# A graph network's raw groups: normalised on VectorE instead of ScalarE, with their statistics taken once a group

## The chip, the cores and the metric

The kernel runs on one core of one Trainium2 chip. The metric is the device time of one execution in microseconds (us); lower is better. The engines are TensorE (PE in the views, its weight loads PEld), VectorE (DVE), ScalarE (ACT), GpSimd (POOL) and SyncE (SP). They run side by side, each in its own program order.

## The reference

One message-passing layer of a graph network with a GRU as the node update: 12500 nodes of 128 features, 400000 edges sorted by destination, 32 features an edge.

```python
h = jnp.maximum(_layernorm(x, axis=-1), 0.0)         # per node
m = relu(concat([h[src], h[dst], ea]) @ w1 + b1) @ w2 + b2
agg = segment_sum(m, dst)                            # 12500 x 128
gi = agg @ w_ih + b_ih;  gh = h @ w_hh + b_hh        # each split into r, z, n
r = sigmoid(i_r + h_r);  z = sigmoid(i_z + h_z);  n = tanh(i_n + r * h_n)
out = x + (1 - z) * n + z * h
```

## The kernel before

**Opening stage** (some 90 us): `x` is loaded in batches, normalised, transposed into `hT_all` (the whole `h`, feature-major, in SBUF), multiplied by the first third of `w1` and stored as the table `A` in HBM, so that for most edges `h[src] @ w1a` is one row of `A`. `B = h @ w1b + b1` is made the same way in batches of 448 nodes.

**Edge stage.** 3125 tiles of 128 edges are worked in 391 groups of 8 tiles (the first has 5), each in two units of 4 tiles: `NU = 782` units. The loop over units runs `stages(u)`, a software pipeline written out by hand: for unit u+3 `pre` multiplies one-hot columns (`L`) with rows of `B` (`RW`) into PSUM, for u+2 `add` adds the source rows, takes the relu and writes `RB` (VectorE, L748), and `seg(u)` multiplies `RB` by one-hot matrices to sum by destination. Every 14 groups a `node` generator does the GRU for a block of nodes, a step a unit.

Source rows reach a group in one of five ways:

- **Groups 0 to 8, "raw"** (`RAW = 9`, units 0 to 17, 69 tiles). `A` isn't stored yet, so GpSimd gathers rows of `x` itself while the opening stage runs. Unit by unit they go through `raw_stats` (VectorE: mean and variance, L227 and L229; ScalarE: the root, L234) at u+7, `raw_fin` (VectorE: six small operations for scale and bias, L240 to L247) and `raw_h` (ScalarE: relu and normalise, one instruction a tile, L292) at u+6, `raw_turn` at u+4 (TensorE transposes into the one PSUM bank `misc`, L699, VectorE copies it to `gt`, L701). `pre` multiplies `gt` by `w1a` (L727). Their relu into `RB` is ScalarE's (L760), once a group.
- **Most of the others**: GpSimd gathers rows of `A`, eight indirect DMAs a group (L170), into a ring of `GBUFS = 11` buffers `G`. A buffer is free when the transposes (raw) or the addition (`A` rows) that reads it are done.
- **31 groups "dve"**: VectorE copies columns of `hT_all` two at a time (`Pairs`, L1021, 512 instructions a group, with loads of addresses into registers between them). `pairs_due` spreads them evenly over the units from `START["dve"]` on; the same number sets which groups they are (18, 30, 42 and so on).
- **30 groups "act"**: ScalarE copies columns one by one (L1062, 1024 a group, spread by `run_jobs`; the first of them, group 11, from unit -6 on).
- **5 groups "sp"**: SyncE issues one small DMA a row.

So each engine's order around the change is fixed by the text of `stages`, by the due counts of the pairs and by the job shares of `run_jobs`; GpSimd's order is the ring.

Of the kernel before, what the change touches and what calls it, by code (L numbers as in the profile page):

```python
# [9 lines left out]
F32 = mybir.dt.float32  # L10
# [7 lines left out]
ALU = mybir.AluOpType  # L18
# [5 lines left out]
GRP = 4  # L24
PAIR = 2 * GRP
# [19 lines left out]
RAW = 9  # L45
# [9 lines left out]
QUEUE = 10  # L55
ROW = 4 * D
SPREAD = {"dve": 31, "act": 30, "sp": 5}
START = {"dve": 8, "act": -6, "sp": 8}
NR = 12672

H_AT = 16512
# [3 lines left out]
def tile_gnn(ctx: ExitStack, tc: tile.TileContext, x, src, srcT, dstT, dstP, eaT, eaP, w1, b1, w2T, b2,  # L65
             wih, bih, whh, bhh, out):
    nc = tc.nc
# [5 lines left out]
    p2 = ctx.enter_context(tc.tile_pool(name="p2", bufs=2))  # L73
# [4 lines left out]
    ps1 = ctx.enter_context(tc.tile_pool(name="ps1", bufs=1, space=bass.MemoryType.PSUM))  # L78
# [7 lines left out]
    def unit_tiles(u):  # L86
        k, h = divmod(u, 2)
        t0, t1 = tiles(k)
        return [(t0 + a * GRP + j, j, a) for j in (2 * h, 2 * h + 1) for a in range(2)
                if t0 + a * GRP + j < t1]  # L90

    mode, order = {}, {m: [] for m in SPREAD}
    for m, n in SPREAD.items():
        lo, hi = START[m] // 2 + 2, NP - {"dve": 5, "act": 3, "sp": 12}[m]
        for i in range(n):
# [32 lines left out]
    ident = const.tile([128, 128], F32, name="ident")  # L128
# [94 lines left out]
    def bn(pool, xs, P, n):  # L223
        b = pool.tile([128, 8, 6], F32, name="bn")
        mv = pool.tile([128, 8, 2], F32, name="mv")
        for j in range(n):
            nc.vector.bn_stats(b[:P, j, :], xs(j))  # L227
        for j in range(n):
            nc.vector.bn_aggr(mv[:P, j, :], b[:P, j, :])  # L229
        return mv  # L230

    def bn_sqrt(pool, mv, P, n):
        s = pool.tile([128, 8], F32, name="s")
        nc.scalar.activation(s[:P, :n], mv[:P, :n, 1], AF.Sqrt, bias=eps[:P, :])  # L234
        return mv, s

    def bn_fin(pool, st, mvs, P, n):
        mv, s = mvs
        y = pool.tile([128, 8], F32, name="y")
        nc.vector.reciprocal(y[:P, :n], s[:P, :n])  # L240
        v = pool.tile([128, 8], F32, name="v")
        nc.vector.tensor_scalar(v[:P, :n], mv[:P, :n, 1], 1e-5, -0.5, op0=ALU.add, op1=ALU.mult)
        nc.vector.tensor_tensor(v[:P, :n], v[:P, :n], y[:P, :n], op=ALU.mult)
        nc.vector.tensor_tensor(v[:P, :n], v[:P, :n], y[:P, :n], op=ALU.mult)
        nc.vector.scalar_tensor_tensor(st[:P, :n, 0], v[:P, :n], 1.5, y[:P, :n],
                                       op0=ALU.add, op1=ALU.mult)
        nc.vector.scalar_tensor_tensor(st[:P, :n, 1], mv[:P, :n, 0], -1.0, st[:P, :n, 0],  # L247
                                       op0=ALU.mult, op1=ALU.mult)
# [42 lines left out]
    def relu_norm(o, xi, st):  # L291
        nc.scalar.activation(o, xi, AF.Relu, bias=st[:, 1:2], scale=st[:, 0:1])  # L292
# [90 lines left out]
    with tc.tile_pool(name="pp", bufs=3) as pp:  # L383
# [22 lines left out]
        mvs, asb = {}, {}  # L406
# [186 lines left out]
    Ls, OH, RT, HE, SEG = ({} for _ in range(5))  # L593
# [14 lines left out]
    def onehot_T(k):  # L608
        if k >= NP:
            return  # L610
        c = slice((k % QP) * 512, (k % QP + 1) * 512)
        o, i = Ls[k // QP][:2 * V, c], Ls[k // QP].bitcast(I32)[:2 * V, c]
        n = k - BLOCKS[-1][0]
        if n < 0:
            nc.vector.tensor_scalar(o, i, node_of[:, k:k + 1], None, op0=ALU.is_equal)  # L615
        else:
            nc.vector.tensor_scalar(o, i, node_of[:, k:k + 1], 0.0, op0=ALU.is_equal, op1=ALU.add,
                                    accum_out=dlast[:2 * V, n:n + 1])
# [50 lines left out]
    def unit(u):  # L669
        k, h = divmod(u, 2)  # L670
        return G[k][:, 2 * h:2 * h + 2, :, :].rearrange("p j a f -> p (j a) f")


    def slots(u):
        return [(j % 2) * 2 + a for _, j, a in unit_tiles(u)]

    def raw_h(u):
        if u < 2 * RAW:
            for i, s in enumerate(slots(u)):
                relu_norm(unit(u)[:, s, :], unit(u)[:, s, :], HE[u][:, i, :])  # L680

    def raw_stats(u):
        if u < 2 * RAW:
            l = slots(u)
            HE[u] = bn_sqrt(p2, bn(p2, lambda j: unit(u)[:, l[j], :], 128, len(l)), 128, len(l))

    def raw_fin(u):
        if u < 2 * RAW:
            n = len(slots(u))
            st = p2.tile([128, GRP, 2], F32, name="st_raw", bufs=4)  # L690
            bn_fin(p2, st[:, :n, :], HE[u], 128, n)
            HE[u] = st

    def raw_turn(u):
        if u < 2 * RAW:
            l = slots(u)
            pt = ps1.tile([128, 512], F32, name="misc")
            for i, s in enumerate(l):
                nc.tensor.transpose(pt[:, i * 128:(i + 1) * 128], unit(u)[:, s, :], ident)  # L699
            hT = p3.tile([128, 512], F32, name="gt", bufs=3)  # L700
            nc.vector.tensor_copy(hT[:, :len(l) * 128], pt[:, :len(l) * 128])  # L701
            HE[u] = hT

    PP = {}
# [1 line left out]
    def pre(u):  # L706
        if u >= NU:
            return
        k, h = divmod(u, 2)
        if h == 0:  # L710
            PP[k] = ps2.tile([128, PAIR, D], F32, name="pre")
        p = PP[k][:, GRP * h:GRP * h + GRP, :]
        for i in range(2):
            c0 = (k % QP) * 512 + (2 * h + i) * 128
            raw = u in HE or k in hand
            nc.tensor.matmul(p[:, 2 * i:2 * i + 2, :], Ls[k // QP][:, c0:c0 + 128], RW[k % 4],  # L716
                             start=True, stop=not raw)
            if raw:
                l = unit_tiles(u)
                for n, (t, j, a) in enumerate(l):  # L720
                    if j % 2 == i:
                        if k in hand:
                            c = (a * GRP + j) * 128
                            cols = hand[k][:, c:c + 128]
                        else:
                            cols = HE[u][:, n * 128:(n + 1) * 128]
                        nc.tensor.matmul(p[:, 2 * i + a, :], cols, w1a, start=False,  # L727
                                         stop=n + 1 == len(l) or l[n + 1][1] != j)
# [28 lines left out]
    def relu(u):  # L757
        if u in RT:
            o, p = RT.pop(u)
            nc.scalar.activation(o, p, AF.Relu)  # L760
# [308 lines left out]
    def pairs_due():  # L1069
        start, n = START["dve"], 0  # L1070
        for k in order["dve"]:
            end = 2 * k - 6
            for u in range(start, end):
                due[u] = n + -(-(PAIR * 64 * (u + 1 - start)) // (end - start))
            n += PAIR * 64
            start = end
# [3 lines left out]
    def behind(u):  # L1080
        return due.get(u, cols.end if u >= START["dve"] else 0) - cols.done

# [4 lines left out]
    def before_long(u, ops):  # L1087
        if u == START["dve"]:
            cols.load()
        some(u, cols.end, QUEUE - ops)  # L1090
        if cols.turn and u % 2 == 0:
            some(u, cols.end, QUEUE - ops - 1)
            cols.part()

    def behind_long(u, least):
        if behind(u) >= least:
            cols.pairs(cols.left())
            cols.load()
# [9 lines left out]
    for m in ("act", "sp"):  # L1108
        start = START[m]
        for k in order[m]:  # L1110
# [39 lines left out]

    def stages(u):
        if u + 7 >= 0:
            raw_stats(u + 7)
        if u + 6 >= 0:
            raw_fin(u + 6)
            raw_h(u + 6)
        if u + 4 >= 0:
            raw_turn(u + 4)
        if u + 3 >= 0:
            pre(u + 3)  # L1160
        before_long(u, 2 if u % 4 == 2 else 1)
        if u % 2 == 0:
            onehot_T(u // 2 + 3)
            onehot(u // 2 + 3)
        if u + 2 >= 0:
            add(u + 2)
            relu(u + 2)
        behind_long(u, 1)

    nc.vector.tensor_scalar(at[:ROWS, :], at[:ROWS, :], place_of[:, 0:1], place_of[:, 1:2],  # L1170
                            op0=ALU.mult, op1=ALU.add)
    for u in range(-7, 0):
        run_jobs(u, 0)
        stages(u)
        for phase in range(1, PH):
            run_jobs(u, phase)
# [16 lines left out]
    for u in range(NU):  # L1193
        k, h = divmod(u, 2)
        gathers(u)
        if h == 0:
# [14 lines left out]
            if k == NP - 20:  # L1211
                check_windows()
        run_jobs(u, 0)
        stages(u)
        run_jobs(u, 1)
        some(u, 4, QUEUE - 1)
# [188 lines left out]
```

## Time and profile before

| | |
|---|---|
| three timed runs | 3355.47, 3372.85, 3372.74 us; median 3372.74 |
| the profiled execution | 3356.5 us; its span 3354.7 us |
| ACT busy | 3232.5 us, 96% of the span |
| POOL busy | 2509.1 us, 75%, 2606 instructions |
| DVE busy | 2429.4 us, 72% |
| PE busy | 2383.9 us, 71%; mean granted clock 0.812 |

Busy shares leave out the loads of registers and the sequencers' own time between two instructions; the views call idle time in which nothing was waited for "issue". So an engine at 75% can be without a pause. The raw groups lie between about 90 and 230 us; everything after them is the long even part, and the last 30 us are the close.

### The profile page before, as it was taken

How to read it: one execution, taken by the hardware profiler on the slowest of the kernel's cores; microseconds unless marked ns; L12 is line 12 of the kernel's file. 1: busy time of each engine (PE TensorE's matmuls, PEld its weight loads, DVE VectorE, ACT ScalarE, POOL GpSimd, SP SyncE). 2: the span in 40 equal slices, each digit the busy share in tenths (PEclk: the TensorE clock that was granted, in tenths of full speed). 3: DMA queues.
4: the chain of work that ended last, by engine and by line, in shares of the span. 5: the costliest groups of instructions: out<-in, count | busy, mean ns of one | idle time of the engine just before them, and what ended most of it. 6: DMA issues, size and time to landing. Idle time of an engine off the chain costs nothing. (4 is left out here: it accounts for less than half of the span.)

```text
span 3354.7 us, 98027 instructions
## 1 busy us (share of the span) xinstructions
PE 2383.9 (71%) x13209; PEld 1538.6 (46%) x13209; DVE 2429.4 (72%) x18411; ACT 3232.5 (96%) x31050; POOL 2509.1 (75%) x2606
## 2 busy tenths in 40 slices
PE   7567777766776777677677676776776676767767
PEld 6444444444444454444444444444444444434444
DVE  8467777777767777777777777767777777777775
ACT  6899999999999999999999999999999999999996
POOL 7657777777777777777777777777777777777776
PEclk9777887878877888778888878877887888888888
DMA  6323444444444443434444344444444434444332
GB/s 212 100 69 84 104 98 102 93 103 99 99 94 100 96 99 94 105 90 98 101 97 100 94 101 99 96 93 101 97 98 100 102 96 95 99 99 100 92 97 72
DMA packets 195246, 332.94 MB, mean 99 GB/s; under 512 B 68682, under 2 KB 117385, under 8 KB 194587
## 3 DMA queue, kind: packets, MB, share of 16 engines
q0 software_dynamic: 83104, 170.36, 23.3%
q1 hardware_dynamic: 111339, 156.21, 17.1%
q14 instruction: 549, 4.50, 0.4%
q8 instruction: 110, 1.80, 0.2%
q10 hardware_dynamic: 144, 0.07, 0.0%
HBM read 306.13 MB, written 20.24 MB: 97 GB/s over the span
## 5 line engine op out<-in xcount | busy, mean ns | idle before, releaser
L1062 ACT COPY HE_act<-hT_all 128x4 uint8 x30720 | 3094.2, 189 | 56.7 <-issue 29.6
L170 POOL DMA_INDIRECT G<-A,src_i x2528 | 2442.0, 966 | 806.0 <-issue 747.7
L1021 DVE SCALAR_TENSOR_TENSOR both<-hT_all 128x4 uint16 x15872 | 1353.8, 153 | 693.6 <-issue 653.6
L716 PE MATMUL pre<-RW,L 128*128 128x256 f32 x3128 | 1101.7, 476 | 9.5 <-DMA RW<-B 9.5
L774 PE MATMUL seg<-RB,OH 128*32 128x129 f32 x6250 | 599.7, 322 | 627.5 <-DVE RB L748 477.6
L716 PEld LDWEIGHTS pre<-RW,L 128*128 128x128 f32 x3128 | 646.3, 231 | 284.3 <-issue 213.1
L774 PEld LDWEIGHTS seg<-RB,OH 128*32 128x32 f32 x6250 | 330.9, 124 | 920.0 <-DVE RB L748 550.9
L748 DVE CUSTOM_DVE_ANT_0 RB<-pre,G 128x1024 f32<-128x1024 f32 (+1 forms) x317 | 383.2, 1209 | 32.0 <-PE pre L716 19.0
L615 DVE TENSOR_SCALAR L<-L,node_of 64x512 f32<-64x512 int32 x382 | 186.7, 489 | 12.0 <-DMA L<-in_dstP 12.0
L666 DVE TENSOR_TENSOR OH<-dloc,seg 128x512 f32<-128x512 f16 (+1 forms) x198 | 131.1, 662 | 0.0
L851 PE MATMUL nd<-DEG,brow 34*128 34x512 f32 (+2 forms) x112 | 72.0, 726 | 82.8 <-ACT gt L861 81.2
L806 PE MATMUL misc<-spot_h,dcol 128*128 128x40 f16 x382 | 47.4, 192 | 88.3 <-DVE dcol L831 86.3
L801 PE MATMUL nd<-spot,sums 128*128 128x40 f32 x782 | 98.7, 290 | 14.2 <-DVE sums L783 12.3
L1032 DVE COPY HE_dve<-both 128x512 uint8<-128x512 uint8 x248 | 107.5, 434 | 0.0
L801 PEld LDWEIGHTS nd<-spot,sums 128*128 128x128 f32 x782 | 93.9, 198 | 22.0 <-DVE sums L783 13.0
L727 PEld LDWEIGHTS pre<-w1a,HE_dve 128*128 128x128 f32 x496 | 87.1, 220 | 9.8
L727 PEld LDWEIGHTS pre<-w1a,HE_act 128*128 128x128 f32 x480 | 84.4, 219 | 14.2 <-ACT HE_act L1062 4.7
L727 PE MATMUL pre<-w1a,HE_act 128*128 128x128 f32 x480 | 84.3, 303 | 4.1 <-ACT HE_act L1062 4.1
L727 PE MATMUL pre<-w1a,HE_dve 128*128 128x128 f32 x496 | 86.1, 302 | 0.0
L806 PEld LDWEIGHTS <-dcol 128*128 128x128 f16 x382 | 38.8, 105 | 101.9 <-DVE dcol L831 93.8
L170 POOL DMA_INDIRECT G<-in_x,src_i x69 | 65.6, 951 | 22.2 <-issue 20.7
L743 DVE TENSOR_SCALAR RB<-pre 128x1024 f32<-128x1024 f32 x61 | 74.0, 1213 | 4.7 <-PE pre L727 4.6
(180 smaller groups left out, 1389.0 us busy)
## 6 DMA issues: line engine op xcount, KB each, us to landing
G_sp<-A SPq DMA_DIRECT2D x5120, 0.5 KB
L<-in_dstP SPq DMA_DIRECT2D x195, 256.0 KB
L<-in_eaP SPq DMA_DIRECT2D x195, 256.0 KB
G<-A,src_i POOLq DMA_INDIRECT x2528, 2.5
RW<-B SPq DMA_DIRECT2D x782, 16.0 KB
xb<-in_x SPq DMA_DIRECT2D x26, 256.0 KB
out<-xb SPq DMA_DIRECT2D x26, 256.0 KB
xs<-in_x SPq DMA_DIRECT2D x11, 512.0 KB
```

Of the source, the lines that this page charges most:

```text
L170: fetched = nc.gpsimd.indirect_dma_start(out=G[k][:, j, a, :], out_offset=None, in_=table, in_offset=bass.IndirectOffsetOnAxis(ap=src_i[c] ...
L615: nc.vector.tensor_scalar(o, i, node_of[:, k:k + 1], None, op0=ALU.is_equal)
L666: nc.vector.tensor_tensor(p, dloc[:, e0:e1, None].to_broadcast(shape), row[:, None, :].to_broadcast(shape), op=ALU.is_equal)
L716: nc.tensor.matmul(p[:, 2 * i:2 * i + 2, :], Ls[k // QP][:, c0:c0 + 128], RW[k % 4], start=True, stop=not raw)
L727: nc.tensor.matmul(p[:, 2 * i + a, :], cols, w1a, start=False, stop=n + 1 == len(l) or l[n + 1][1] != j)
L748: made = nc.vector._custom_dve(TENSOR_ADD_SAT, out=o, in0=p, in1=G[k].rearrange("p j a f -> p (j a) f")[:, c, :], s0=float("inf"), s1=0.0)
L774: nc.tensor.matmul(p[r0:r0 + V, :D + 1], OH[k][:, a * GRP + j, :], RB[k % 2][:, 2 * j + a, :D + 1], start=False, stop=all(b != a for _, _, ...
L801: nc.tensor.matmul(p[:, bass.ds(offs[i], V + SHIFT)], sums[:, slot(b, i), :D], spot[:, i % 2, :], start=False, stop=i == len(offs) - 1)
L806: nc.tensor.matmul(p[:, bass.ds(offs[i], V + SHIFT)], t[:, c:c + 128], spot_h[:, a, :], start=False, stop=i == len(offs) - 1)
L1021: nc.vector.scalar_tensor_tensor(self.both[:, e % PIECE // 2, :], column(second), 256.0, column(first), op0=ALU.mult, op1=ALU.add)
L1032: nc.vector.tensor_copy(hand[k].bitcast(U8)[:, p0 * 4:(p0 + PIECE) * 4].rearrange("p (n c b) -> p n c b", c=2, b=4), both.bitcast(U8).rear ...
L1062: nc.scalar.copy(he[:, e * 4:e * 4 + 4], column(v))
```

## The change

The statistics of a raw group are now ended once a group (eight tiles) rather than once a unit: `raw_stats(u + 8)` on even units, the root `raw_sqrt(u + 7)` one unit later and ahead of it in the text, `raw_fin(u + 6)` once a group. `raw_h` is a VectorE `tensor_scalar` (times scale plus bias, no relu) a tile; the relu moves into the copy behind the transposes, which becomes `tensor_scalar` with max and moves from `raw_turn` to `raw_copy` at the end of the stage. `START["dve"]` goes from 8 to 10: the pairs begin two units later, and 15 of the 31 "dve" groups become the next group (18 becomes 19), with three "act" and one "sp" group giving way by one.

```diff
-START = {"dve": 8, "act": -6, "sp": 8}
+START = {"dve": 10, "act": -6, "sp": 8}
...
+    def raw_stats(u):
+        if u % 2 == 0 and u < 2 * RAW:
+            l = [(v, s) for v in (u, u + 1) for s in slots(v)]
+            HE[u] = bn(p2, lambda i: unit(l[i][0])[:, l[i][1], :], 128, len(l)), len(l)
+
+    def raw_sqrt(u):
+        if u % 2 == 0 and u < 2 * RAW:
+            mv, n = HE[u]
+            HE[u] = bn_sqrt(p2, mv, 128, n), n
...
     def raw_h(u):
         if u < 2 * RAW:
             for i, s in enumerate(slots(u)):
-                relu_norm(unit(u)[:, s, :], unit(u)[:, s, :], HE[u][:, i, :])
...
+                nc.vector.tensor_scalar(unit(u)[:, s, :], unit(u)[:, s, :], HE[u][:, i, 0:1], HE[u][:, i, 1:2],
+                                        op0=ALU.mult, op1=ALU.add)
...
+    def raw_copy(u):
+        if u < 2 * RAW:
+            n = len(slots(u)) * 128
             hT = p3.tile([128, 512], F32, name="gt", bufs=3)
-            nc.vector.tensor_copy(hT[:, :len(l) * 128], pt[:, :len(l) * 128])
+            nc.vector.tensor_scalar(hT[:, :n], HE[u][:, :n], 0.0, None, op0=ALU.max)
...
     def stages(u):
         if u + 7 >= 0:
-            raw_stats(u + 7)
+            raw_sqrt(u + 7)
+        raw_stats(u + 8)
         if u + 6 >= 0:
             raw_fin(u + 6)
             raw_h(u + 6)
@@ -1165,10 +1176,13 @@
         if u + 2 >= 0:
             add(u + 2)
             relu(u + 2)
+        if u + 4 >= 0:
+            raw_copy(u + 4)
         behind_long(u, 1)
```

On ScalarE, in the middle of the raw groups, a unit before is a root (L234), four normalisations (L292), after every second unit the relu of a group (L760), and copies of columns (L1062) between:

```order
L234 ACTIVATE s<-mv,eps 128x4
L292 ACTIVATE G<-G,st_raw 128x128 x4
L760 ACTIVATE RB_179<-pre 128x8x128
L1049 TENSOR_LOAD at
L1062 COPY HE_act<-hT_all 128x4 x16
L1049 TENSOR_LOAD at
L1062 COPY HE_act<-hT_all 128x4 x16
L1049 TENSOR_LOAD at
L1062 COPY HE_act<-hT_all 128x4 x12
L234 ACTIVATE s<-mv,eps 128x4
L292 ACTIVATE G<-G,st_raw 128x128 x4
```

The same place after, with the relu and the copies under their new line numbers:

```order
L1072 COPY HE_act<-hT_all 128x4 x16
L1059 TENSOR_LOAD at
L1072 COPY HE_act<-hT_all 128x4 x16
L234 ACTIVATE s<-mv,eps 128x8
L770 ACTIVATE RB_179<-pre 128x8x128
L1059 TENSOR_LOAD at
L1072 COPY HE_act<-hT_all 128x4 x16
```

The normalisations are gone from ScalarE and one root of eight columns stands where two of four stood. The relu is the next step on ScalarE that needs TensorE (`pre`).

On VectorE, two units before are twice the chain of statistics, the small operations and the copy `gt`, shown here once:

```order
L227 BN_STATS bn<-G 128x6 x4
L229 BN_AGGR mv<-bn 128x2 x4
L240 RECIPROCAL y<-s 128x4
L242 TENSOR_SCALAR v<-mv 128x4
L243 TENSOR_TENSOR v<-v,y 128x4
L244 TENSOR_TENSOR v<-v,y 128x4
L245 SCALAR_TENSOR_TENSOR st_raw<-v,y 128x4
L247 SCALAR_TENSOR_TENSOR st_raw<-mv,st_raw 128x4
L701 COPY gt<-misc 128x512
```

Two units after, behind statistics of eight tiles (L227 and L229 x8), with one chain of eight and the normalisations (L697) among the rest; the copies (L711) stand at the end of each stage:

```order
L240 RECIPROCAL y<-s 128x8
L242 TENSOR_SCALAR v<-mv 128x8
L243 TENSOR_TENSOR v<-v,y 128x8
L244 TENSOR_TENSOR v<-v,y 128x8
L245 SCALAR_TENSOR_TENSOR st_raw<-v,y 128x8
L247 SCALAR_TENSOR_TENSOR st_raw<-mv,st_raw 128x8
L697 TENSOR_SCALAR G<-G,st_raw 128x128 x4
L615 TENSOR_SCALAR L<-L,node_of 64x512
L666 TENSOR_TENSOR OH_185<-dloc,seg_80 128x512
L711 TENSOR_SCALAR gt<-misc 128x512
L697 TENSOR_SCALAR G<-G,st_raw 128x128 x4
L711 TENSOR_SCALAR gt<-misc 128x512
```

The root that the reciprocal (L240) reads was asked for a unit earlier, on statistics that ended a unit before that, so VectorE has other work between asking and using it.

More of the change, by code (lines that the diff above doesn't have):

```diff
@@ L675, in slots, with raw_fin @@
         return [(j % 2) * 2 + a for _, j, a in unit_tiles(u)]
+    def raw_stats(u):
[6 more added lines that the diff above has]
+            HE[u] = bn_sqrt(p2, mv, 128, n), n
+    def raw_fin(u):
+        if u % 2 == 0 and u < 2 * RAW:
+            mvs, n = HE[u]
+            st = p2.tile([128, PAIR, 2], F32, name="st_raw")
+            bn_fin(p2, st[:, :n, :], mvs, 128, n)
+            HE[u], HE[u + 1] = st[:, :len(slots(u)), :], st[:, len(slots(u)):, :]
     def raw_h(u):
@@ L679, in raw_h @@
             for i, s in enumerate(slots(u)):
-                relu_norm(unit(u)[:, s, :], unit(u)[:, s, :], HE[u][:, i, :])
[L682 to L692, printed above, removed]
+                nc.vector.tensor_scalar(unit(u)[:, s, :], unit(u)[:, s, :], HE[u][:, i, 0:1], HE[u][:, i, 1:2],
+                                        op0=ALU.mult, op1=ALU.add)
     def raw_turn(u):
@@ L696, in raw_turn @@
             l = slots(u)
-            pt = ps1.tile([128, 512], F32, name="misc")
+            HE[u] = ps1.tile([128, 512], F32, name="misc")
             for i, s in enumerate(l):
-                nc.tensor.transpose(pt[:, i * 128:(i + 1) * 128], unit(u)[:, s, :], ident)
+                nc.tensor.transpose(HE[u][:, i * 128:(i + 1) * 128], unit(u)[:, s, :], ident)
+    def raw_copy(u):
+        if u < 2 * RAW:
+            n = len(slots(u)) * 128
             hT = p3.tile([128, 512], F32, name="gt", bufs=3)
-            nc.vector.tensor_copy(hT[:, :len(l) * 128], pt[:, :len(l) * 128])
+            nc.vector.tensor_scalar(hT[:, :n], HE[u][:, :n], 0.0, None, op0=ALU.max)
             HE[u] = hT
@@ L1171, in tile_gnn @@
                             op0=ALU.mult, op1=ALU.add)
+    raw_stats(0)
     for u in range(-7, 0):
```

## The prediction

> **What bounds the kernel now.** I read the page first, for the shares, then the waits of GpSimd, and then the order of time around the raw groups and at the close.
>
> ```profile
> span 3354.7 us, 98027 instructions
> L1062 ACT COPY HE_act<-hT_all 128x4 uint8 x30720 | 3094.2, 189 | 56.7 <-issue 29.6
> POOL G L170 <- issue: 768.5, 2519, 0.6
> POOL G L170 <- DVE RB L748: 21.5, 18, 12.1
> POOL G L170 <- PE misc L699: 16.1, 5, 4.0
> ```
>
> ScalarE's copies alone are 3094.2 us of a span of 3354.7. GpSimd looks idler, but 768.5 us of its idle time are pauses of 0.3 us behind 2519 gathers, in which nothing is waited for: with 0.94 us for the gather itself (the row at 3337.08 below) one comes every 1.25 us, and GpSimd has next to nothing to spare. What it truly waits for is a free buffer, and that is short: 16.1 us on the transposes of raw groups and 21.5 on additions, less the usual 0.3 each time (5 and 18 times): 14.6 + 16.1 = 31 us. The order of time says where they lie, and who is last at the end.
>
> ```profile
> 231.38 0.95 POOL L170 DMA_INDIRECT G<-A,src_i  x1 [12.06 <-DVE RB L748]
> 265.83 0.95 POOL L170 DMA_INDIRECT G<-A,src_i  x1 [1.91 <-DVE RB L748]
> 3337.08 0.94 POOL L170 DMA_INDIRECT G<-A,src_i  x1 [0.30 <-issue]
> 3339.72 0.69 DVE L748 CUSTOM_DVE_ANT_0 RB<-pre,G 128x512 f32<-128x512 f32 x1 [4.04 <-DMA G<-A,src_i]
> 3321.62 3.58 ACT L1062 COPY HE_act<-hT_all 128x4 uint8 x36
> ```
>
> The longest wait is at 231 us, where the first ordinary group (9) gives its buffer to the twelfth; the last of note is at 265.83. From there GpSimd gathers without a pause to 3337.08, and the very last addition (3339.72) waits 4.04 us for its rows. ScalarE's last copy ends at 3325.2. So GpSimd's chain closes the kernel and ScalarE's ends close before it. Both were set back in the raw groups, the only place where the change acts.
>
> ```profile
> 103.65 0.30 ACT L234 ACTIVATE s<-mv,eps 128x4 f32<-128x4 f32 x1 [4.61 <-DVE mv L229]
> 121.40 0.29 ACT L234 ACTIVATE s<-mv,eps 128x4 f32<-128x4 f32 x1
> 121.60 1.63 ACT L292 ACTIVATE G<-G,st_raw 128x128 f32<-128x128 f32 x4
> 123.14 3.96 ACT L1062 COPY HE_act<-hT_all 128x4 uint8 x40
> 128.74 1.00 ACT L760 ACTIVATE RB<-pre 128x1024 f32<-128x1024 f32 x1
> 191.00 0.29 ACT L234 ACTIVATE s<-mv,eps 128x4 f32<-128x4 f32 x1
> ```
>
> In the raw groups ScalarE has no pause after 104 us: each unit holds a root (0.20 from start to start), four normalisations (123.14 - 121.60 = 1.54) and some 42 copies. VectorE waits for it there:
>
> ```profile
> 174.11 0.86 DVE L227 BATCH_NORM_STATS2 bn<-G 128x6 f32<-128x128 f32 x4
> 174.89 0.36 DVE L229 BATCH_NORM_AGGREGATE mv<-bn 128x2 f32<-128x6 f32 x4
> 178.62 0.18 DVE L240 RECIPROCAL y<-s 128x4 f32<-128x4 f32 x1 [3.37 <-ACT s L234]
> 179.56 0.68 DVE L701 COPY gt<-misc 128x512 f32<-128x512 f32 x1
> ```
>
> A unit's statistics are over at 175.25, their root comes at 178.6 behind the copies.
>
> **The change part by part. ScalarE.** It loses 69 normalisations, 1.54 us for four, 26.6 us in all, and 9 of 18 roots at 0.20, 1.8 us. The wait of 4.61 us goes too, since the statistics then stand ahead of VectorE's wait for `L`. But the start of the chain stays where it is, as TensorE and the DMA show:
>
> ```profile
> 101.73 0.48 DVE L615 TENSOR_SCALAR L<-L,node_of 64x512 f32<-64x512 int32 x1 [9.55 <-DMA L<-in_dstP]
> 117.15 1.19 PE L716 MATMUL pre<-RW,L 128*128 128x256 f32 x2 [9.45 <-DMA RW<-B]
> 122.25 0.38 PE L727 MATMUL pre<-w1a,gt 128*128 128x128 f32 x2
> ```
>
> `pre` of unit 0 waits for rows of `B` until 117.15, whatever the other engines do, and unit 1 of it is done at 122.6. ScalarE's relu of group 0 can't start before that; it started at 128.74. ScalarE would be there 12.1 us earlier, at 116.6 (the wait of 4.6 us, 18 tiles of units 1 to 5 at 1.54 / 4, three roots); it turns the difference into a new wait for TensorE, and only 128.7 - 122.6 = 6.1 us are won up to the relu. From the relu to the last root, asked at 191.00, the stretch was 62.3 us; without nine units of normalisations (13.9) and five roots (1.0) it is 47.4. The last root is then asked at 170.0 rather than 191.0.
>
> **VectorE.** It gains 69 `tensor_scalar` of 128x128. The trace has none; the nearest rows bound it:
>
> ```profile
> L227 DVE BATCH_NORM_STATS2 bn<-G 128x6 f32<-128x128 f32 x69 | 14.9, 273 | 0.0
> L615 DVE TENSOR_SCALAR L<-L,node_of 64x512 f32<-64x512 int32 x20 | 9.6, 479 | 9.6 <-DMA L<-in_dstP 9.6
> L242 DVE TENSOR_SCALAR v<-mv 128x4 f32<-128x4 f32 x16 | 2.6, 163 | 0.0
> L666 DVE TENSOR_TENSOR OH<-dloc,seg 128x512 f32<-128x512 f16 x9 | 6.0, 670 | 0.0
> L783 DVE COPY sums<-seg 128x129 f32<-128x129 f32 x8 | 2.2, 280 | 0.0
> ```
>
> In the first three rows, the same operation takes 0.163 us on 4 columns and 0.479 on 512; 128 columns lie at 0.163 + 0.316 x 124 / 508 = 0.24. The ends are 0.163 and the 0.273 of a statistics operation of this very shape. At 0.24, less the overlap, I take 0.2 from start to start: 0.8 us a unit, 14 us in all. Nine chains of the six small operations go, each 179.56 - 178.62 = 0.94, 8.5 us. The copy with max keeps its 0.68. In the raw units VectorE's own work is about 3.7 us a unit (2.2 + 0.9 + 1.6 + 1.4 for two units, and 1.1 for `L`, half an `OH` and the sums) against ScalarE's 4.8 (42.7 copies of 0.10, a root and a relu every second unit), so this is covered by ScalarE; if the cover were gone, it would cost the 14 - 8.5 = 5.5 us.
>
> What follows the raw groups isn't covered:
>
> ```profile
> 198.51 0.18 DVE L240 RECIPROCAL y<-s 128x4 f32<-128x4 f32 x1 [1.41 <-ACT s L234]
> 182.03 0.60 DVE L1021 SCALAR_TENSOR_TENSOR both<-hT_all 128x4 uint16 x7 [1.79 <-issue]
> 229.89 1.21 DVE L748 CUSTOM_DVE_ANT_0 RB<-pre,G 128x1024 f32<-128x1024 f32 x1
> L1021 DVE SCALAR_TENSOR_TENSOR both<-hT_all 128x4 uint16 x215 | 17.8, 152 | 12.8 <-issue 12.8
> ```
>
> From the first pairs (unit 8, 182.03 less its load of addresses: 180.2) to the addition of group 9 at 229.89, VectorE waits once for another engine, 1.41 us. The 49.7 us are its own program: 215 pairs at (17.8 + 12.8) / 215 = 0.142 us and the rest. Here VectorE, not ScalarE, sets when buffers come free. After the change this piece starts at unit 10: the root at 170.0, the chain 0.9, four normalisations 0.8, so at 171.8. It is shorter by the wait (1.4), two units of statistics (2.2), three chains (2.8), a copy (0.6), and by pairs: 512 spread over 22 units are 23.3 a unit, so with the start two units later 47 fewer are done by then, 6.7 us. Small steps of the other units go both ways, under 1 us, and aren't counted. 49.7 - 13.7 = 36.0: the addition of group 9 comes at 207.8 rather than 229.9, **22 us earlier**.
>
> **GpSimd.** Without its waits on the transposes it could be at group 22 some 14.6 us earlier, at 231.4 - 11.8 - 14.6 = 205.0, and now waits there to about 209. The next three buffers (groups 10, 12, 13) come from additions 22 us earlier as well, so that at 265.83 GpSimd is 22 us early, and from there on it has no wait to lose or win. Its order changes by one group (18 is gathered, 19 not); the count of gathers is the same. SyncE's queue gives `L` and `RW` in the old order, by buffers that are free earlier.
>
> **The close.** ScalarE is some 25 us early (6.1 + 13.9 + 1.0 and three more units, 4.6), GpSimd 22. The pairs were put off by 6.7 us of work which VectorE has to make up over the remaining units; it has waits to do it in:
>
> ```profile
> DVE gt L865 <- ACT gt L861: 40.7, 11, 6.2
> ```
>
> 40.7 us it waits for ScalarE's gates. So the end moves with GpSimd: 3356.5 - 22 = 3334.5 us on the footing of the profiled execution. That execution and one timed run (3355.47) stand 17 us below the other two (3372.85, 3372.74), and nothing in one trace tells me what parts them. I put the forecast on the mean of the four, 3364.4, which lies 8.3 under the median: 3364.4 - 22 = 3342 us.
>
> **A rule that speaks against it.** GpSimd's gathers and VectorE's new operations may collide, and the trace shows both outcomes:
>
> ```profile
> 101.83 1.19 POOL L170 DMA_INDIRECT G<-A,src_i  x1 [0.30 <-issue]
> 128.55 0.94 POOL L170 DMA_INDIRECT G<-A,src_i  x1 [0.30 <-issue]
> 128.87 0.47 DVE L615 TENSOR_SCALAR L<-L,node_of 64x512 f32<-64x512 int32 x1
> ```
>
> The gather at 101.83 runs beside the `tensor_scalar` of 101.73 and takes 0.25 us longer than usual; the one at 128.55 runs beside the same operation and doesn't. So a `tensor_scalar` costs GpSimd between nothing and 0.25 us; taking half of its length at half of the times, 69 x 0.24 / 4 = 4 us, which falls before group 22, where GpSimd has 4 us of waiting left. The Trainium skill, page "SBUF — State Buffer", section "Who interferes with whom", says that `tensor_scalar` with operands in SBUF can take both of VectorE's ports, that GpSimd shares the second pair, and that the later of the two is blocked for the whole of the other's instruction; by it every overlap costs. This trace agrees at 101.83 and not at 128.55.
>
> **The rivals.**
>
> *Less: collision.* If each of the 69 normalisations holds GpSimd up for its full 0.24 us, that is 16.6 us; 4 are absorbed at group 22, and 12.6 come off: a gain of 9, 3355 us. For it: 101.83. Against it: 128.55. The rule of the page just named would give this case. Chance 0.09.
>
> *Less: the pairs.* If VectorE, not GpSimd, sets the pace to the end, the 6.7 us of pairs come back: a gain of 15, 3349 us. For it: VectorE's unbroken stretch around 230 us. Against: the 40.7 us it waits for ScalarE. Chance 0.12.
>
> *More.* If VectorE frees buffers so early that GpSimd loses all its 31 us of waits, the end moves by 31: 3333 us. For it: GpSimd's chain closes the kernel. Against: `pre` can't start before 117.15. Chance 0.10.
>
> *Slower: VectorE and TensorE take turns.* The copy `gt` now stands at the end of VectorE's stage, and TensorE's next transposes wait for it, for there is one bank `misc`. A unit of TensorE at a low clock is long:
>
> ```profile
> 133.09 1.11 PE L699 MATMUL misc<-ident,G 128*128 128x128 f32 x4 [0.64 <-DVE brow L549]
> 137.54 0.95 PE L774 MATMUL seg<-RB,OH 128*32 128x129 f32 x4
> ```
>
> From 133.09 to 138.49 it takes 5.4 us. If nothing of that overlapped VectorE's 3.7, a raw unit would take 9.1; eleven units from the relu at 122.6 end at 222.7 rather than 171.8 and the addition of group 9 comes at 258.7, 29 us late: 3393 us. It turns slower once a raw unit is over about 6.5 us, since 22 us on 11 units are 2.0 each beyond 4.5. Against it: `pre` and `seg` need not wait for VectorE's next stage. Chance 0.11.
>
> **How the numbers follow.** The forecast, 22 us with 17 to 28 as its ends, has 0.58. A measurement of this kernel can tell about 0.5%, 17 us, from no change. Faster by more: 0.58 + 0.10 = 0.68. Within: 0.12 + 0.09 = 0.21. Slower: 0.11. The range takes in both footings: from 31 us off the lower (3355 - 31 = 3324) to 15 off the upper (3373 - 15 = 3358). It leaves out the slower case and part of the collision, under 0.2.
>
> **What would show it.** Right: no L292 on `G`; ScalarE waits for TensorE before its first L760 and then has raw units of about 4.8 us; the reciprocal no longer waits; GpSimd's waits on transposes are gone and those on additions near 231 us are small; the addition of group 9 stands near 208. Wrong: gathers beside the normalisations stretched to 1.2 us throughout; VectorE waiting at each `gt` copy; or the last gather ending early with another engine closing the kernel.

## The result and the profile after

| | before | after |
|---|---|---|
| median of the timed runs | 3367.73 us (3355.47 to 3372.85, 4 runs) | 3342.83 us (3335.17 to 3345.27, 4 runs) |
| the profiled execution | 3356.5 us | 3335.17 us |

The four runs after include the profiled execution, those before don't. The ratio is 0.9917, with a 95% interval of 0.9896 to 0.9939: 24.9 us less in the medians, 21.3 in the profiled executions. Measured again (experiment 1) it was 0.9918 (0.9903 to 0.9934).

The page after, and from the list of waits those of GpSimd, ScalarE and VectorE that the argument needs (waited for: total us, times, longest):

```profile
span 3333.4 us, 97941 instructions
L1072 ACT COPY HE_act<-hT_all 128x4 uint8 x30720 | 3091.8, 189 | 52.4 <-issue 24.4
```

```profile
POOL G L170 <- issue: 763.9, 2504, 0.6
DVE gt L875 <- ACT gt L871: 28.1, 13, 5.5
POOL G L170 <- DVE RB L758: 14.0, 16, 5.1
DVE y L240 <- ACT s L234: 12.3, 8, 3.4
ACT RB L770 <- PE pre L737: 9.2, 1, 9.2
POOL G L170 <- PE misc L705: 2.6, 1, 2.6
```

GpSimd's waits for buffers fell from 21.5 and 16.1 us to 14.0 and 2.6. ScalarE has one new wait, 9.2 us for `pre`. VectorE still waits 12.3 us for roots, and 28.1 for ScalarE's gates, 40.7 before. The order of time shows where these lie: ScalarE and VectorE in the raw groups, GpSimd's waits, and the close.

```profile
119.00 1.19 PE L726 MATMUL pre<-RW,L 128*128 128x256 f32 x2 [9.25 <-DMA RW<-B]
124.72 1.02 ACT L770 ACTIVATE RB<-pre 128x1024 f32<-128x1024 f32 x1 [9.24 <-PE pre L737]
125.40 0.94 POOL L170 DMA_INDIRECT G<-A,src_i  x1 [2.64 <-PE misc L705]
163.38 0.30 ACT L234 ACTIVATE s<-mv,eps 128x8 f32<-128x8 f32 x1
172.89 0.30 ACT L234 ACTIVATE s<-mv,eps 128x8 f32<-128x8 f32 x1
173.22 0.20 DVE L240 RECIPROCAL y<-s 128x8 f32<-128x8 f32 x1 [3.36 <-ACT s L234]
201.21 1.01 ACT L770 ACTIVATE RB<-pre 128x1024 f32<-128x1024 f32 x1
210.14 1.21 DVE L758 CUSTOM_DVE_ANT_0 RB<-pre,G 128x1024 f32<-128x1024 f32 x1
211.63 0.94 POOL L170 DMA_INDIRECT G<-A,src_i  x1 [5.11 <-DVE RB L758]
246.12 0.94 POOL L170 DMA_INDIRECT G<-A,src_i  x1 [1.93 <-DVE RB L758]
3299.22 3.57 ACT L1072 COPY HE_act<-hT_all 128x4 uint8 x36
3313.43 0.94 POOL L170 DMA_INDIRECT G<-A,src_i  x1 [0.31 <-issue]
3316.07 0.69 DVE L758 CUSTOM_DVE_ANT_0 RB<-pre,G 128x512 f32<-128x512 f32 x1 [2.76 <-DMA G<-A,src_i]
```

The last relu of a raw group, which stands here at 201.21, stood before at:

```profile
224.04 1.01 ACT L760 ACTIVATE RB<-pre 128x1024 f32<-128x1024 f32 x1
```

Read it from the top. TensorE still waits for rows of `B`, until 119.00. ScalarE is ready 9.24 us ahead of `pre`. The roots then come every 9.5 us (163.38 to 172.89), 4.8 a unit. The root of the last raw group is asked for at 172.89; before, that group had two, at 191.00 and 197.95. Group 9 is added at 210.14 rather than 229.89. The wait of GpSimd at 231.38, 12.06 us long before, stands at 211.63 with 5.11. Its last wait of note is at 246.12 rather than 265.83: 19.7 us are won there. Its last gather is 23.65 us earlier (3313.43 against 3337.08), the last instruction 21.3. The very last addition waits for gathered rows as before, 2.76 us. ScalarE's last relu of a raw group is 22.8 us earlier, and its last copy ends 22.4 earlier (3302.79 against 3325.20). So the time was won in the first 250 us, at the raw groups, and carried to the end.

### The profile page after: what moved, and what is told of

Read it like the earlier page. It is cut to its first block, busy times and chain, and to the rows that moved or that the text cites. A ratio compares the mean times of both kernels' runs of the same rounds, so it can differ in the third digit from the quotient of the medians.

```text
span 3333.4 us, 97941 instructions
## 1 busy us (share of the span) xinstructions
PE 2384.4 (72%) x13209; PEld 1540.3 (46%) x13209; DVE 2442.7 (73%) x18426; ACT 3202.7 (96%) x30972; POOL 2506.4 (75%) x2606
## 5 line engine op out<-in xcount | busy, mean ns | idle before, releaser
L1072 ACT COPY HE_act<-hT_all 128x4 uint8 x30720 | 3091.8, 189 | 52.4 <-issue 24.4
L1031 DVE SCALAR_TENSOR_TENSOR both<-hT_all 128x4 uint16 x15872 | 1356.0, 153 | 687.5 <-issue 646.5
L811 PEld LDWEIGHTS nd<-spot,sums 128*128 128x128 f32 x782 | 96.4, 202 | 18.9 <-DVE sums L793 11.6
```

Source lines behind the costliest of these rows:

```text
L811: nc.tensor.matmul(p[:, bass.ds(offs[i], V + SHIFT)], sums[:, slot(b, i), :D], spot[:, i % 2, :], start=False, stop=i == len(offs) - 1)
L1031: nc.vector.scalar_tensor_tensor(self.both[:, e % PIECE // 2, :], column(second), 256.0, column(first), op0=ALU.mult, op1=ALU.add)
L1072: nc.scalar.copy(he[:, e * 4:e * 4 + 4], column(v))
```

## The experiments

All start from the changed kernel, and each ratio is to the kernel before on the same chip. They ran in three rounds, each on a chip of its own: 1 to 4, 5 to 8 and 9 to 12. Timed runs are set beside each other only within a round.

**1. The changed kernel again**, no edit.

> The changed kernel again, as the measure for the other runs of this chip: about 0.992 of the kernel before by every theory.

Measured: 3344.63 us against 3372.64, ratio 0.9918 (0.9903 to 0.9934): 28.0 us. The result stands, and the next three runs share its chip.

**2. The normalisations back on ScalarE**, all the rest as changed.

```diff
-                nc.vector.tensor_scalar(unit(u)[:, s, :], unit(u)[:, s, :], HE[u][:, i, 0:1], HE[u][:, i, 1:2],
-                                        op0=ALU.mult, op1=ALU.add)
+                relu_norm(unit(u)[:, s, :], unit(u)[:, s, :], HE[u][:, i, :])
```

> The changed kernel with one part undone: the normalisations are ScalarE's again, the statistics once a group, the early roots and the late copies stay. If ScalarE's load paces the raw groups (my theory): 21 of the 69 tiles fall into its new wait of 9 us for the first relu and cost nothing, the rest costs 1.54 us a unit; the last root is asked some 14 us later than at 172.9, group 9 is added near 224 and the end is 14 us later than the changed kernel, 0.998 of the kernel before. If the early roots are what helped (rival: VectorE's waits of 33 us for the roots): within 4 us of the changed kernel, 0.993.

Measured: 3364.29 us, ratio 0.9977 (0.9968 to 0.9985), 19.7 us above experiment 1. Its order of time:

```profile
125.43 1.00 ACT L769 ACTIVATE RB<-pre 128x1024 f32<-128x1024 f32 x1
186.71 0.30 ACT L234 ACTIVATE s<-mv,eps 128x8 f32<-128x8 f32 x1
219.72 1.01 ACT L769 ACTIVATE RB<-pre 128x1024 f32<-128x1024 f32 x1
222.58 1.22 DVE L757 CUSTOM_DVE_ANT_0 RB<-pre,G 128x1024 f32<-128x1024 f32 x1
224.06 0.94 POOL L170 DMA_INDIRECT G<-A,src_i  x1 [9.61 <-DVE RB L757]
258.53 0.94 POOL L170 DMA_INDIRECT G<-A,src_i  x1 [1.58 <-DVE RB L757]
3329.98 0.95 POOL L170 DMA_INDIRECT G<-A,src_i  x1 [0.31 <-issue]
3333.63 1.29 DVE L757 CUSTOM_DVE_ANT_0 RB<-pre,G 128x512 f32<-128x512 f32 x2 [3.04 <-PE pre L725]
```

The relu has no wait for `pre`: ScalarE comes there just late enough. Between relu and last root lie 61.3 us (186.71 - 125.43) rather than 48.2 (172.89 - 124.72), 13.1 more for nine units of normalisations; the forecast had 13.9 for them. Group 9 is added 12.4 us later, and GpSimd's last wait lies 12.4 us later too (258.53 against 246.12). The end was expected 14 us later and is 19.7 later, more than GpSimd's wait explains. ScalarE explains it: behind the last root three units of normalisations follow, its last relu of a raw group comes 18.5 us later (219.72 against 201.21), and its last copy ends 18.6 later (3321.42 against 3302.79). GpSimd's last gather is done 23.2 us before the end, where in experiment 1 it was 18.9, and the last additions wait for `pre` and not for rows. So with the normalisations on ScalarE its chain fits the end better than GpSimd's. In the timed runs their move makes 19.7 of the 28.0 us, and the rest of the change 8.4. The rival, that the earlier roots win the time and the place of the normalisations matters little, falls as the main cause.

**3. `START["dve"]` back to 8.**

```diff
-START = {"dve": 10, "act": -6, "sp": 8}
+START = {"dve": 8, "act": -6, "sp": 8}
```

> The changed kernel with START of the pairs back at 8. My theory: 47 pairs more stand ahead of the addition of group 9, which comes 6.7 us later, near 217; GpSimd waits there 12 us rather than 5, and since it closes the kernel the end is 5 to 7 us later, 0.994 of the kernel before. If the pairs put off are repaid before the end: no difference to the changed kernel. If the later start of the pairs were the whole of the gain: 1.00.

Measured: 3345.41 us, ratio 0.9923 (0.9908 to 0.9938), which the timed runs can't tell from experiment 1. In its trace the last reciprocal (at 175.30) has no wait, and group 9 is added 2.6 us later than after:

```profile
212.73 1.21 DVE L758 CUSTOM_DVE_ANT_0 RB<-pre,G 128x1024 f32<-128x1024 f32 x1
214.21 0.94 POOL L170 DMA_INDIRECT G<-A,src_i  x1 [8.28 <-DVE RB L758]
```

The 47 pairs that stand ahead of the addition again don't cost their 6.7 us. From 172.89 to the addition there are 188 of them, 21 more than after; the others come before that, where they can fill waits for roots such as the 3.36 us that the changed kernel has ahead of 173.22. Only 2.6 us are left. The 5 to 7 us that the theory expected at the end are missing, and no difference at all, as if the pairs were made up for later, isn't ruled out. A later start of the pairs is at most a small part of the gain.

**4. The rows of `B` for the first units asked for sooner.** Before the loop, SyncE's queue had three groups of source rows and `L` ahead of the four `RW`; now each group's `RW` go ahead of the next group's fetch.

```diff
-    for q in range(3):
+    fetch(0)
+    for q in range(1, 3):
+        window_rows(2 * q - 2)
+        window_rows(2 * q - 1)
         fetch(q)
-    for k in range(4):
-        window_rows(k)
```

> The changed kernel with the first rows of B asked for ahead of the second and third L on SyncE's queue. My theory: pre of unit 0 no longer waits until 119 but starts near 106 to 109, ScalarE's wait of 9.2 us at its first relu goes, all that follows in the raw groups is 7 to 9 us earlier, GpSimd's waits of 2.6, 5.1, 3.0 and 1.9 us go, and the end is 7 to 10 us earlier than the changed kernel, 0.989 of the kernel before. If ScalarE's own work to the end or the later L set the pace: within 2 us of the changed kernel.

Measured: 3336.17 us, ratio 0.9896 (0.9881 to 0.9912), 8.5 us below experiment 1 in the medians.

```profile
108.68 1.06 PE L726 MATMUL pre<-RW,L 128*128 128x256 f32 x2
116.03 1.00 ACT L770 ACTIVATE RB<-pre 128x1024 f32<-128x1024 f32 x1
163.99 0.30 ACT L234 ACTIVATE s<-mv,eps 128x8 f32<-128x8 f32 x1
201.05 1.21 DVE L758 CUSTOM_DVE_ANT_0 RB<-pre,G 128x1024 f32<-128x1024 f32 x1
236.93 0.94 POOL L170 DMA_INDIRECT G<-A,src_i  x1 [1.93 <-DVE RB L758]
3302.84 0.95 POOL L170 DMA_INDIRECT G<-A,src_i  x1 [0.30 <-issue]
```

`pre` starts at 108.68 with no wait for `RW`, the relu at 116.03 with no wait for `pre`, 8.7 us earlier. The 8.7 pass from step to step: 8.9 at the last root, 9.1 at group 9's addition, 9.2 at GpSimd's last wait. ScalarE's last relu of a raw group is 8.9 earlier as well (192.31). Of GpSimd's waits, which were all expected to go, 1.2 us at 225.28 and 1.9 at 236.93 are left. This is the chain of the forecast, moved by a different push, and it is the fastest version found.

**5 to 8. Four variants on a slow chip.** These ran on a chip on which every kernel took about 1.77 times as long (before: 5952.37 us; granted clock 0.66 to 0.67 in all runs, rather than 0.80 to 0.81). Statistics and roots once a unit with VectorE normalising (as in 11 below):

> The changed kernel with the statistics, roots and small operations of before: once a unit, the root asked in the stage that ends the statistics and used in the next; the normalisations stay on VectorE. If ScalarE's normalisations were the matter (my theory): nine more roots cost ScalarE 1.8 us and nine more chains cost VectorE 8.5 us, most of it in its waits for roots (8.4 us behind 125 us); the end is 2 to 5 us later than the changed kernel, 0.993 of the kernel before. If the early roots are half of the gain (rival): VectorE waits some 1 us or more for each of 18 roots and the end is 10 us or more later, 0.995 or above.

Measured 5942.36 us, ratio 0.9985 (0.9975 to 0.9995). The copy `gt` right behind the transposes rather than at the stage's end (`raw_copy(u + 4)` moved up to `raw_turn(u + 4)`):

> The changed kernel with the copy of the turned tiles back right behind the transposes, in the middle of the stage. My theory: VectorE waits about 1 us for each turn, in time in which it would have waited for roots; 0 to 2 us, 0.992 of the kernel before. If the copy's place at the stage's end is what keeps VectorE and TensorE from taking turns (rival): 18 waits of 1 us that aren't covered, 8 us or more later.

Measured 5942.7 us, ratio 0.9976 (0.9966 to 0.9987). Six "sp" groups rather than five (9 below):

> The changed kernel with six groups rather than five brought by SyncE, so eight gathers fewer on GpSimd, 10 us; the work of ScalarE and VectorE stays. If GpSimd closes the kernel (my theory): the end is 5 to 9 us earlier, until ScalarE's last copies come next, 0.990 of the kernel before. If ScalarE closes it (rival): no difference to the changed kernel.

Measured 5893.67 us, ratio 0.9909 (0.9896 to 0.9922). Each normalisation followed by a second, neutral one (10 below):

> The changed kernel with each of the 69 normalisations followed by a second tensor_scalar of the same form (times 1 plus 0), 17.8 us more on VectorE at 0.258 us each. My theory, VectorE has cover in the raw groups: 21 of them fall into its wait for TensorE ahead of 123 us, the other 48 cost 12.4 us of which 8.4 fall into its waits for roots; group 9 is added and the kernel ends some 4 us later, 0.993 of the kernel before. If there is no cover (rival): 15 to 18 us later, 0.997. If the normalisations hold up GpSimd's gathers, those of the raw stretch get longer by up to 0.25 us each.

Measured 5941.67 us, ratio 0.9983 (0.9971 to 0.9995). None answers its question by its time, since another thing bounds the kernel there, as the waits of the second of them show:

```profile
POOL G L170 <- DVE RB L758: 2437.1, 220, 50.1
ACT HE_act L1072 <- issue: 2268.8, 3079, 1.9
```

GpSimd waits 2437.1 us for buffers, where after it was 14.0. ScalarE's copies have 2268.8 us of pauses with nothing waited for, where after it was 24.4, and VectorE's pairs 1839.3 (646.5). Both engines copy columns at addresses that they load into registers; ScalarE's loads take 1.04 us each, as on the other chip, and what makes the pauses, the trace doesn't show. Where GpSimd waits that much throughout, what a change in the raw groups gives it isn't carried to the end. Six "sp" groups are some 48 us faster there than the other three variants; the cause isn't shown. The place of the `gt` copy was asked only here: in that trace 17 of the 18 copies start without a wait and one waits 1.2 us, so the waits of 1 us a turn that both theories took for granted aren't there. On an ordinary chip the question stays open.

**9. Six "sp" groups**, on a chip of ordinary speed again (before: 3358.99 us). One group of gathers less on GpSimd was to show whether GpSimd closes the kernel.

```diff
-SPREAD = {"dve": 31, "act": 30, "sp": 5}
+SPREAD = {"dve": 31, "act": 30, "sp": 6}
```

> Six groups rather than five brought by SyncE, so eight gathers fewer on GpSimd, 10 us; the work of ScalarE and VectorE stays. On a chip with the times of the first runs: if GpSimd closes the kernel (my theory), the end is 5 to 9 us earlier than the changed kernel, until ScalarE's last copies come next, 0.990 of the kernel before. If ScalarE closes it (rival): no difference to the changed kernel, 0.992.

Measured: 3643.63 us, ratio 1.0846 (1.0831 to 1.0861). All expectations missed. Its waits:

```profile
DVE L L615 <- DMA L<-in_dstP: 311.6, 107, 8.1
POOL G L170 <- DVE RB L758: 265.5, 63, 20.7
SPq L107 <- PE pre L726: 111.3, 30, 11.4
```

The changed kernel's SyncE:

```profile
SPq L107 <- PE pre L726: 237.4, 64, 16.8
```

These waits are most of what SyncE had to give, 237.4 us. With 1024 more row DMAs (6144 rather than 5120) they fall to 111.3, and `L`, which stands in the same queue, comes late 107 times. VectorE, and behind it GpSimd, wait for it. SyncE had little to spare either, and this run can't tell who closes the kernel: there ScalarE too waits 299 us for others between its last raw relu and its last copy.

**10. Each normalisation twice**, the second with scale 1 and bias 0 from a constant tile `one_zero`.

```diff
+                nc.vector.tensor_scalar(unit(u)[:, s, :], unit(u)[:, s, :], one_zero[:, 0:1], one_zero[:, 1:2],
+                                        op0=ALU.mult, op1=ALU.add)
```

> Each of the 69 normalisations followed by a second tensor_scalar of the same form (times 1 plus 0), 17.8 us more on VectorE at 0.258 us each. On a chip with the times of the first runs: with cover in the raw groups (my theory) group 9 is added and the kernel ends some 4 us later than the changed kernel, 0.993 of the kernel before; without cover (rival) 15 to 18 us later, 0.997. If the normalisations hold up GpSimd's gathers, those of the raw stretch get longer by up to 0.25 us each.

Measured: 3345.01 us, ratio 0.9962 (0.9947 to 0.9976). The pairs of operations on VectorE, GpSimd's waits, and its gathers in the raw groups (the last row groups the window from 93 to 250 us: busy us and mean ns of one, idle us before them):

```profile
152.87 0.34 DVE L700 TENSOR_SCALAR G<-G,st_raw 128x128 f32<-128x128 f32 x1
153.25 0.57 DVE L702 TENSOR_SCALAR G<-G,one_zero 128x128 f32<-128x128 f32 x1
153.51 0.38 DVE L700 TENSOR_SCALAR G<-G,st_raw 128x128 f32<-128x128 f32 x1
...
224.03 0.94 POOL L170 DMA_INDIRECT G<-A,src_i  x1 [12.29 <-DVE RB L763]
258.23 0.94 POOL L170 DMA_INDIRECT G<-A,src_i  x1 [1.60 <-DVE RB L763]
```

```profile
L170 POOL DMA_INDIRECT G<-A,src_i x107 | 102.5, 958 | 58.1 <-issue 27.4 <-DVE RB L763 15.2 <-PE misc L710 9.3
```

A pair comes every 0.64 us (152.87 to 153.51), where one normalisation alone takes 0.26: the second works on the first's result and starts only when that has ended (153.25, after 152.87 + 0.34). For the 48 tiles of six groups from the relu on that is 0.38 x 48 = 18.2 us more on VectorE. GpSimd's last wait is 12.1 us later than after (258.23 against 246.12). So some 6 us were covered, and not more: there was cover, as the theory said, but 4 us at the end were expected and the ratio lies nearer to the 0.997 of the rival. The expectation priced the second operation like the first. ScalarE now waits for `pre` in the raw groups, 6.0 us ahead of four relus, and its last one comes at 208.15, 6.9 us later. The gathers, at 958 ns, aren't longer than after (961).

**11. Statistics, roots and small operations once a unit as before**, normalising on VectorE.

```diff
-        if u % 2 == 0 and u < 2 * RAW:
-            l = [(v, s) for v in (u, u + 1) for s in slots(v)]
-            HE[u] = bn(p2, lambda i: unit(l[i][0])[:, l[i][1], :], 128, len(l)), len(l)
+        if u < 2 * RAW:
+            l = slots(u)
+            HE[u] = bn_sqrt(p2, bn(p2, lambda j: unit(u)[:, l[j], :], 128, len(l)), 128, len(l))
...
-            raw_sqrt(u + 7)
-        raw_stats(u + 8)
+            raw_stats(u + 7)
...
```

> The changed kernel with the statistics, roots and small operations of before, once a unit; the normalisations stay on VectorE. On a chip with the times of the first runs: if ScalarE's normalisations were the matter (my theory), 2 to 5 us later than the changed kernel, 0.993 of the kernel before. If the early roots are half of the gain (rival): 10 us or more later, 0.995 or above.

Measured: 3337.77 us, ratio 0.9938 (0.9925 to 0.9952).

```profile
213.67 0.95 POOL L170 DMA_INDIRECT G<-A,src_i  x1 [7.60 <-DVE RB L753]
248.16 0.94 POOL L170 DMA_INDIRECT G<-A,src_i  x1 [1.59 <-DVE RB L753]
```

GpSimd's last wait is 2.0 us later than after (248.16 against 246.12), and the longest is 7.60 rather than 5.11. So by the traces the grouping into eights and the roots asked for a unit ahead are worth some 2 us there. The ratio fits the 2 to 5 us of the theory and lies below the rival's 0.995, though its interval just reaches that. The changed kernel itself wasn't timed in this round, so the timed runs give no figure of their own.

**12. The fastest version with six "sp" groups** (4 and 9 together).

> The changed kernel with the first rows of B asked for ahead of the second and third L, and with six groups brought by SyncE: both steps that the theory calls gains. If GpSimd closes the kernel, the gains of 8.5 and of 5 to 9 us add up only as far as ScalarE lets them: 3 to 9 us earlier than with the first step alone, 0.987 to 0.989 of the kernel before. If ScalarE is as late as GpSimd by then: 0.9896, as with the first step alone.

Measured: 3627.38 us, ratio 1.0804 (1.0787 to 1.082): experiment 9's loss again, lowered by 16 us. The fastest version stays that of experiment 4.

## Why the prediction was right

The forecast was 3342 us (3324 to 3358), from a gain of 22 us; the median is 3342.83. That the two agree to 1 us is luck: the footing of 3364.4 was 3.3 us below the median before, 3367.73, and the gain 2.9 below the 24.9 of the medians. The mechanism came as forecast up to 250 us. Which engine carries it to the end is less certain than the forecast had it. Step by step:

**ScalarE's new wait** came where it was put, before the first relu of a raw group, for `pre`, with TensorE waiting for `RW`. It was forecast for 122.6 and came at 124.72, since the rows of `B` landed at 119.00 rather than 117.15. That this held the start is shown by experiment 4, where the rows come sooner and everything behind moves with them.

**The stretch from relu to last root** was 48.2 us, forecast 47.4. The root at 191.00 that the forecast calls the last is the first of the last group's two; it stands where the group's only root stands now, so the sum isn't touched. ScalarE has no wait from the relu at 124.72 on, so its copies set the pace here and VectorE's normalisations lie under it.

**The normalisation's price** was outside its bounds. The forecast took 0.24 us from ends of 0.163 and 0.273, and 0.2 from start to start. The trace has 0.340 as the middle value (shortest, median and longest in ns):

```profile
L697 DVE TENSOR_SCALAR G<-G,st_raw x69: 324/340/553, 94.1 to 181.5; 128x128 f32<-128x128 f32 x69
```

And in the order of time:

```profile
106.70 1.11 DVE L697 TENSOR_SCALAR G<-G,st_raw 128x128 f32<-128x128 f32 x4
107.73 0.47 DVE L615 TENSOR_SCALAR L<-L,node_of 64x512 f32<-64x512 int32 x1
```

Four of them take 1.03 us to the next operation, 0.26 each. The interpolation went between operations with one such scalar or none (`L` compares with one column, `node_of`); this one takes scale and bias from two columns of a tile. It made no difference, as the 4 us more (69 x 0.06) lie under ScalarE's pace.

**VectorE behind the last root.** The forecast gave 37.8 us from the root to the addition of group 9; it took 37.25 (210.14 - 172.89). Pairs, as counted in the two stretches (before from 178.62, after from 172.89, to the addition of group 9):

```profile
L1021 DVE SCALAR_TENSOR_TENSOR both<-hT_all 128x4 uint16 x215 | 17.8, 152 | 12.8 <-issue 12.8
```

```profile
L1031 DVE SCALAR_TENSOR_TENSOR both<-hT_all 128x4 uint16 x167 | 14.2, 154 | 10.1 <-issue 10.1
```

48 fewer, where 47 were forecast. The addition is thus 2.3 us later than forecast (210.14, not 207.8): 2.1 from the relu and 0.8 from the stretch behind it, less 0.5 here. What the step misjudged is only what it put down to `START`: with 8, two further units of pairs would partly have filled the 3.36 us and the like that VectorE waits ahead of roots, so that the later start is worth 2.6 us at this addition (experiment 3) and not 6.7.

**GpSimd.** A wait of 4 us was forecast at group 22, and 5.1 measured. Its waits on transposes were to go; one was left (2.64 at 125.40), behind the late `pre`. From its last wait on it runs without one to the end: 3071.3 us from there to the last gather before, 3067.3 after, 3071.5 in experiment 2, 3065.9 in 4, and between 3064.4 and 3073.1 in every run on an ordinary chip with five "sp" groups. So what GpSimd has won by 250 us arrives at its last gather, give or take 4 us.

**Who closes the kernel.** The forecast said GpSimd, and that isn't shown. ScalarE's chain runs just as full: between its last relu of a raw group and its last copy, 3098.6 to 3107.5 us later, it waits for other engines only 1.0 to 13.0 us in all. All traces on ordinary chips with five "sp" groups, in us:

| | GpSimd's last wait ends | ScalarE's last raw relu | span | from the wait to the end | from the relu to the end |
|---|---|---|---|---|---|
| before | 265.83 | 224.04 | 3354.7 | 3088.9 | 3130.7 |
| after | 246.12 | 201.21 | 3333.4 | 3087.3 | 3132.2 |
| experiment 1 | 246.18 | 201.26 | 3329.5 | 3083.3 | 3128.3 |
| 2, normalisations on ScalarE | 258.53 | 219.72 | 3353.2 | 3094.7 | 3133.5 |
| 3, pairs from 8 on | 248.66 | 201.22 | 3331.3 | 3082.7 | 3130.1 |
| 4, rows of `B` sooner | 236.93 | 192.31 | 3320.6 | 3083.6 | 3128.3 |
| 10, each twice | 258.23 | 208.15 | 3341.2 | 3083.0 | 3133.0 |
| 11, statistics once a unit | 248.16 | 202.12 | 3339.1 | 3090.9 | 3137.0 |

The last column spreads by 8.7 us, the one before it by 12.0. The two chains part most in experiment 2, which moves them by 12.4 and 18.5 us against after; the end moves by 19.8 there (23.7 against experiment 1, 19.7 in the timed medians), which fits ScalarE. For GpSimd speaks that the very last addition waits for its rows in all of them but experiment 2. The run that was to part the two failed (9). The forecast came out all the same, as the change moved both chains by nearly as much: 22 and some 25 us forecast, 19.7 and 22.8 measured, and 21.3 at the end of the profiled executions. Why the medians show 24.9 and 28.0 isn't traced further.

**The rivals.** *Collision:* the gathers in the raw groups (93 to 250 us after, 93 to 270 before) took 961 ns on average after and 952 before, which on 115 of them is 1 us, not 16.6:

```profile
L170 POOL DMA_INDIRECT G<-A,src_i x115 | 110.5, 961 | 49.5 <-issue 32.0 <-DVE RB L758 10.0 <-DMA A<-asb 3.1
```

```profile
L170 POOL DMA_INDIRECT G<-A,src_i x116 | 110.4, 952 | 70.4 <-issue 32.6 <-DVE RB L748 16.9 <-PE misc L699 16.1
```

Single ones are longer (1.53 us at 147.94). With twice the normalisations the mean was 958. The Trainium skill, page "SBUF — State Buffer", section "Who interferes with whom", has the later of the two engines blocked for the whole of the other's instruction where VectorE takes both pairs of ports. No run shows whether these operations do; at that price the gathers beside them don't bear it out. *The pairs paid back at the end:* the end moved by 21.3 us, between the 19.7 and 22.8 of the two chains, so no sign of it. *VectorE and TensorE in turns:* a raw unit took 4.8 us, as forecast, not 9.1. *More:* GpSimd kept 16.6 us of its waits, 11.5 without the usual 0.3 each time, so the 31 weren't reached; experiment 4 shows the way there, sooner rows of `B`, as the argument against that rival said.

**The footing.** A mean of four executions was taken, as nothing told what parted them. That served, but what parts them is still not shown (last section).

## What to carry to other kernels

When several engines are nearly full, find every chain that runs without a pause to the end, and ask when each last waits: what a change ahead of that point saves can only reach the end as far as all of these chains move. Here there were two, and one wait alone misled: in experiment 2 GpSimd's moved by 12.4 us and the end by 19.7. Give work to an engine that waits for the one you relieve, and add up both per step first: here some 6 us of cover were left on VectorE, and a second operation on each tile moved GpSimd's last wait by 12. Whatever you relieve will next wait for something else (here rows of `B`, late in a queue), and moving that up was worth 8.5 us more, beside a gain of 28.0.

## What was not expected of the hardware

- In the first measurement and in experiments 1 to 4 the profiled execution is the fastest of its kernel, by 6 to 14 us (after 3335.17 against 3342.64 to 3345.27; experiment 4: 3322.34 against 3336.07 to 3338.20), and in experiments 9 to 11 it isn't (experiment 10: 3342.96, the others 3341.15 to 3354.98). In the first times one of the timed runs was as fast as the profiled execution (3355.47 and 3356.5). So what makes the gap of 17 us isn't shown.
- The same program took 1.77 times as long on one chip, with pauses of up to 1.9 us between ScalarE's copies, 2268.8 us in all (experiment 6). This kernel, balanced between engines on one chip, has another bound there.
- Here a `tensor_scalar` of 128x128 with scale and bias from columns of a tile took 0.34 us, 0.26 from start to start; one that needs the result of the one before added 0.38.
- SyncE was nearly full too: with 1024 more row DMAs of 0.5 KB on its queue the kernel took 285 us more than before, gain and all.
